# A planned MetaFormer layer on one core: the set-up work of the pipeline's filling, split and put elsewhere

## The chip, the cores and the metric

The kernel runs on one core of a Trainium2 chip. The metric is the device time of one execution in microseconds. The kernel before took 2755.74 us, the median of three runs (2751.01 to 2756.01). A core has five engines that work side by side, each in the order of its own instruction list: TensorE (PE, matmul; its weight loads are PEld), VectorE (DVE), ScalarE (ACT), GpSimd (POOL) and SyncE (SP). SP issues most transfers here, ACT the stores of intermediate results. An instruction waits, where it must, on semaphores, and everything behind it on the same engine waits with it.

## The reference

One layer over x of shape (8, 128, 128, 96): a Fourier token mixer, then a feed-forward network that rounds to small floats. What matters here:

```
x = x + conv(ln_c(x))                      # token mixer
t = x + ffn(ln_t(x))                       # 96 -> 384 -> 96
conv: x_pre = soa(ln(x) @ w1)              # 192 channels, relu, squared
      xf    = rfft2(x_pre)                 # per channel, over 128 x 128
      filt  = three filters, (16,9), (8,4), (24,13) coefficients,
              enlarged by cubic interpolation to (128, 65)
      r     = softmax(mlp(means of the image))    # mixes the three filters
      out   = irfft2(xf * sum(filt * r)) @ w2
ffn:  y = q_acc(q_acc(q_mul(x) @ q_mul(W)) + q_mul(b))   # q_mul: 5 exponent, 2 mantissa bits
```

All matmuls of the mixer are in float32. Everything that depends only on the parameters (the projection with batch norm folded in, the filters' enlarged rows, the rounded weights of the network) is computed on the chip at the start of each execution.

## The kernel before, in words

Each of the eight images goes through three streams. Stream a (`before`, the first pass): blocks of 16 columns are loaded (`load_x`, L802), their statistics taken (`measure`, L748; `variance`, `root`, `inverse`, `rest`, L753 to L782), the factors stored to DRAM (`store_r`, L815, buffer Rd) and loaded again spread over 96 partitions (`load_r`, L819, buffer rB, two of them). A transposed copy of x (`load_xT`, L811, four buffers zT with a row of ones below, so that the bias comes in with the matmul) is scaled by them (`scale`, L823), projected (`project`, L836, px), rectified and squared on ACT (L847, L854), transformed along one axis (`transform`, L865, py), folded on DVE (`fold`, L877, yst) and stored by ACT (`store_y`, L881, buffer Yd). When a whole image is through, its rates follow (`rate_v0` to `rate_n`). Stream s (`spectrum`) loads Yd and the filter rows T again, transforms along the other axis (`along_w`, L1059, pz), weighs and multiplies with the filters, mixes channels and transforms back. Stream c (`after`) finishes the inverse, adds the residual and runs the network. The streams of different images overlap; at the start there is only stream a of image 0.

The order is not that of the program text. Every step is handed to `at(time, function, ..., after=...)` with a wished place in time and the steps that it needs. `in_order` then walks through a model of the five engines, with the costs of the table `COST` (engine, time on it, time of its transfers), and takes on each engine the step that is ready and has the best score of place and delay. The outcome is a fixed order of instructions for every engine. The places of the streams come from `WINDOWS` and `OFFSETS`; the places of the set-up work from three constants, `T_WEIGHTS`, `T_CONST` and `T_ROWS`, on the same scale.

The set-up work is of four kinds. `make_weights` (L622) folds batch norm into the projection W1S (DVE, ACT, POOL and one matmul) and clears the ones rows of the four zT (`nc.gpsimd.memset`, L637). `others` (L639) makes small constants after eleven loads (L554). `rows` and `ends` (L682, L663) make the filters' rows with small matmuls; `row_put` and `end_put` (L690, L673) copy them out on DVE and, in the same step, issue two stores to T from SP (L695, L696, L678). `weights` (L698) issues four loads of the network's parameters from SP (L705 to L709) and, in the same step, six casts on DVE (L710 to L715). Since a step is put into the order as one, its loads stand on SP and its casts on DVE at the place where the planner took it.

A buffer that is to be filled again makes its new writer wait for the last reader: two of rB, two of xb, six of tk (row copies), two of te (end copies). Each transfer also waits, on its issuing engine, for an earlier transfer that used the same of eight completion semaphores.

Of the kernel before, what the change touches and what calls it, by code (L numbers as in the profile page):

```python
# [34 lines left out]
F32 = mybir.dt.float32  # L35
# [7 lines left out]
B, H, W, C = 8, 128, 128, 96  # L43
# [5 lines left out]
HID = 384  # L49
NHC = HID // 128  # L50
# [4 lines left out]
R = 2 * NW  # L55
# [7 lines left out]
NU = W // QW  # L63
PAIRS = [w for u in range(NU) for w in (2 * u, 2 * u + 1, 127 - 2 * u, 126 - 2 * u)]

T_WEIGHTS, T_CONST, T_ROWS = -112.0, 40.0, (-19.0, 94.0)

WINDOWS = {
    "a": ((-1016.3, 224.2), (1155.2, 782.6), (913.1, 640.2), (700.4, 97.1), (81, 722.9), (986.1, 683.8), (1759.7, 398.2), (2087.9, 538.4)),
    "s": ((159.4, 351.5), (85.6, 1024.7), (720.2, 346.4), (425.8, 331.2), (-126.3, 469.9), (-78, 205.3), (815.2, 257), (1827.2, 30.5)),  # L70
    "c": ((1028.7, 511.2), (1109.6, 188.3), (1290.9, 349.7), (1829.2, 439.1), (2176.6, 456.9), (2490.5, 149.5), (2420.5, 484.7), (2163.8, 1143.1)),
}
OFFSETS = {
    "a_context": -69.32,
# [19 lines left out]
    "a_root": -155.19,  # L94
    "a_scale": 83.17,
    "a_square": 92.51,
    "a_store_r": 12.56,
    "a_store_y": -218.91,
    "a_transform": -124.2,
    "a_variance": -11.06,  # L100
    "c_accumulated": -194.42,
    "c_add_up": -42.25,
    "c_bias": -232.6,
    "c_biased": -34.16,
    "c_first": -3.46,
# [6 lines left out]
    "c_measure": 206.09,  # L112
    "c_put8": 55.17,
    "c_quantise": 161.11,
    "c_quantise_v": 271.29,
    "c_residual": -76.16,
    "c_rest": -195.99,
    "c_root": 122.09,
# [8 lines left out]
    "s_alone_z": 223.71,  # L127
    "s_along_w": -28.38,
    "s_combine": -31.52,
    "s_copy_sr": 135.72,  # L130
    "s_filters_of": 27.98,
    "s_invert": 0.86,
    "s_inverted": -111.88,
# [22 lines left out]
PE, ACT, DVE, POOL, SP = range(5)  # L156
# [60 lines left out]
    "a_rate_n": (DVE, 4, 0),  # L217
    "_make_weights": (DVE, 7.4, 0),
    "_others": (DVE, 1.5, 1),
    "_weights": (DVE, 5, 2),  # L220
    "_ends": (PE, 2.2, 0),
    "_end_put": (DVE, 1.25, 1),
    "_rows": (PE, 1.2, 0),
    "_row_put": (DVE, 1.25, 1),
    "_next_pool": (SP, 0, 0),
    "a_load_x": (SP, 0.6, 1.92),
    "a_load_xT": (SP, 0.8, 1.05),
# [303 lines left out]
def metaformer_kernel(ctx: ExitStack, tc: tile.TileContext, a: dict, out: bass.AP):  # L531
    nc = tc.nc
# [11 lines left out]
    ops = []  # L544
# [61 lines left out]
    def projection(sp):  # L606


        raw = sp.tile([C, MED + SCTX + RHID], F32, name="raw")
        ident = sp.tile([128, 128], F32, name="ident")  # L610
        CEN = load(T_WEIGHTS, "CEN", [C, C], pool=sp)
        row = [C + 1, SCTX]
        bn = load(T_WEIGHTS, "bn", [C + 1, 4, SCTX], a["bn"].partition_broadcast(C + 1), sp)
        var, gam, mu, bet = (bn[:, i, :] for i in range(4))
        soa_scale = load(T_WEIGHTS, "soa1_scale", [128, 1], a["soa1_scale"].partition_broadcast(128), sp)
        bn_a = sp.tile(row, F32, name="bn_a")
        bn_t = sp.tile(row, F32, name="bn_t")

        def load_raw():
            nc.sync.dma_start(out=raw, in_=a["raw"])  # L620

        def make_weights():  # L622
            nc.vector.tensor_scalar(var, var, 1e-5, None, ALU.add)
            rsqrt(bn_a, var, bn_t)
            nc.vector.tensor_tensor(bn_a, bn_a, gam, ALU.mult)
            nc.vector.tensor_tensor(mu, mu, bn_a, ALU.mult)
            nc.vector.tensor_tensor(mu, bet, mu, ALU.subtract)
            pr = bank("pr")
            nc.tensor.matmul(pr[:C, : MED + SCTX + RHID], lhsT=CEN, rhs=raw, start=True, stop=True)
            nc.scalar.copy(W1S[:C, :MED], pr[:C, :MED])  # L630
            nc.vector.tensor_tensor(W1S[:C, MED:], pr[:C, MED : MED + SCTX], bn_a[:C, :], ALU.mult)
            nc.vector.memset(W1S[C:, :MED], 0.0)
            nc.vector.tensor_copy(W1S[C:, MED:], mu[C:, :])
            nc.scalar.copy(fc1a, pr[:C, MED + SCTX : MED + SCTX + RHID])
            nc.vector.tensor_scalar(F1, F1, soa_scale, None, ALU.mult)
            for t in zTs:
                nc.gpsimd.memset(t[C : C + 1, :, :], 1.0)  # L637

        def others():  # L639
            nc.vector.tensor_scalar(w2N, w2C, -1.0, None, ALU.mult)  # L640
            make_identity(nc, ident)
            nc.vector.tensor_copy(ident8, ident, saturate=False)
            nc.vector.memset(ones, 1.0 / (H * W))
            nc.vector.tensor_scalar(soa_bias, soa_bias, 128.0, None, ALU.mult)

        at(T_WEIGHTS, load_raw)
        loads = ("CEN", "bn", "soa1_scale", "F1", "load_raw")
        at(T_WEIGHTS + 0.1, make_weights, after=[(None, k) for k in loads], banks=1, until=[(None, "make_weights")])
        at(T_CONST, others, after=[(None, "soa1_bias"), (None, "w2C")])

    def filters(sp):
# [21 lines left out]
        def end_put(s, q):  # L673
            tk = sp.tile([L, 2, MED], F32, name="te", tag="te", bufs=2)
            nc.vector.tensor_copy(tk.rearrange("k r m -> k (r m)"), pts.pop(("end", s, q)))
            r0 = R + 4 * s + 2 * q
            for i in range(2):
                nc.sync.dma_start(out=T[i, r0 : r0 + 2, :, :].rearrange("r k m -> k r m"), in_=tk)  # L678

        pts = {}  # L680
# [9 lines left out]
        def row_put(i, s):  # L690
            (_, c, w0, n) = next(p for p in pieces[i] if p[0] == s)
            tk = sp.tile([128, 2, MED], F32, name="tk", tag="tk", bufs=6)
            nc.vector.tensor_copy(tk[:, :n, :].rearrange("k r m -> k (r m)"), pts.pop((i, s)))
            r0 = c * NW + WOFF[s] + w0
            nc.sync.dma_start(out=T[0, r0 : r0 + n, :, :].rearrange("r k m -> k r m"), in_=tk[:L, :n, :])  # L695
            nc.sync.dma_start(out=T[1, r0 : r0 + n, 1 : L - 1, :].rearrange("r k m -> k r m"), in_=tk[L:, :n, :])  # L696

        def weights():  # L698
            w1f = sp.tile([C, HID], F32, name="w1f")
            w2f = sp.tile([128, NHC, C], F32, name="w2f")  # L700
            b1f = sp.tile([128, NHC], F32, name="b1f")
            b2f = sp.tile([128, C], F32, name="b2f")
            b1h = sp.tile([128, NHC], F8, name="b1h")
            b2h = sp.tile([128, C], F8, name="b2h")
            nc.sync.dma_start(out=w1f, in_=a["W1T"])  # L705
            nc.sync.dma_start(out=w2f, in_=a["W2T"].rearrange("(n p) c -> p n c", p=128))
            with nc.allow_non_contiguous_dma("384 biases"):
                nc.sync.dma_start(out=b1f, in_=a["b1"].rearrange("(n p) -> p n", p=128))
            nc.sync.dma_start(out=b2f, in_=a["b2"].partition_broadcast(128))  # L709
            nc.vector.tensor_copy(W1q, w1f, saturate=False)  # L710
            nc.vector.tensor_copy(W2q, w2f, saturate=False)
            nc.vector.tensor_copy(b1h, b1f, saturate=False)
            nc.vector.tensor_copy(b2h, b2f, saturate=False)
            nc.vector.tensor_copy(b1q, b1h.unsqueeze(2).to_broadcast([128, NHC, QW * 128]))
            nc.vector.tensor_copy(b2q, b2h)  # L715
# [4 lines left out]
        ]  # L720
        n = max(len(p) for p in by_scale)
        pieces = [[p[i] for p in by_scale if i < len(p)] for i in range(n)]
        for i in range(n):
            t = T_ROWS[0] + (T_ROWS[1] - T_ROWS[0]) * i / n
            puts = [(None, "row_put", i, p[0]) for p in pieces[i]]
            at(t, rows, i, after=[(None, "load_scales")], banks=len(puts), until=puts)
            for k in puts:
                at(t + 1, row_put, i, k[3], after=[(None, "rows", i)])
        for s in range(NS):
            t = T_ROWS[1] + 1 + s  # L730
            puts = [(None, "end_put", s, q) for q in range(2)]
            at(t, ends, s, after=[(None, "load_scales")], banks=2, until=puts)
            for q in range(2):
                at(t + 0.5, end_put, s, q, after=[(None, "ends", s)])
        at(T_ROWS[1] + 5, weights, after=[(None, "row_put", n - 1, 2)])

    def named(what, b, n):

# [50 lines left out]
    def before(b, t0, P):  # L789
# [97 lines left out]
        for u in range(NU):  # L887
# [10 lines left out]
            if q % 2 == 0:  # L898
                hb = u // 2
                after = both("project", u - 2 * NZT) + both("project", u - 2 * NZT + 1)  # L900
                if b == 0:
                    after.append((None, "make_weights"))
                at(t - 0.003, load_xT, hb, after=after)
                at(t, load_r, hb, after=[one("scale", hb - 2), one("store_r", blk)])
                after = [one("load_xT", hb), one("load_r", hb)]
                at(t, scale, hb, after=after)
# [101 lines left out]
    def spectrum(b, t0, P):  # L1008
# [200 lines left out]
            kept_v[b] += 1  # L1209

        stored_y = [(("a", b), "store_y", u) for u in range(NU)]
        filled = [op.key for op in ops if b == 0 and op.key[1] in ("row_put", "end_put", "others", "GL", "GM", "SEL")]

        def mixer(g):

# [236 lines left out]
        pools["c"] = ctx.enter_context(tc.tile_pool(name="pc", bufs=2))  # L1452

    stream[0] = None
    at(T_ROWS[1] + 6, next_pool, after=[op.key for op in ops if op.key[0] is None])
    for op, banks in in_order(in_turn(ops)):
        free_banks[:] = banks
        op.what(*op.args)
# [52 lines left out]
```

## Time and profile before

| what | value |
|---|---|
| median of three runs | 2755.74 us (2751.01 to 2756.01) |
| the profiled execution's own time | 2760.28 us |
| its span in the profile | 2758.4 us |
| mean clock granted to PE | 0.942 |
| PE, DVE, ACT, POOL busy | 89%, 83%, 78%, 61% of the span |
| moved by transfers | 621.17 MB, 225 GB/s in the mean |
| first scaling (L823) | 34.85 us |
| first fold (L877) | 50.19 us |
| rates of image 0 begin (L928) | 211.28 us |
| first matmul of stream s (L1059) | 242.10 us |

The profile shows one execution. All times in it are microseconds from the span's start. A row of a group or of the order of time names the line of the kernel, the engine, the operation, the tile written and the tile read, and how many instructions it holds; the idle time before it stands in brackets, with what ended it. "SPq" and "ACTq" are the issuing of transfers. A stage's row gives for each engine the busy time in it, then the clock granted to PE as a share of the full one, the mean busy share of the 16 transfer engines and what they moved.

### The profile page before, as it was taken

The page shows a single profiled execution, that of the slowest core. Times are in us where ns is not written, and L with a number is a line of the kernel's source. Part 1 is how long each engine was busy: PE and PEld are TensorE (multiplying, and loading weights), DVE is VectorE, ACT ScalarE, POOL GpSimd, SP SyncE. Part 2 cuts the span into 40 slices and gives each one's busy share as a digit, 9 for nine tenths or more (in the row PEclk, how much of TensorE's full clock was granted, in tenths as well). Part 3 has the DMA queues.
Part 4 walks back from the last instruction along what each step waited for, and adds up shares of the span by engine and source line. Part 5 has one row for each costly group of instructions (what it writes and reads, how often), then busy time and mean ns, then how long its engine had stood idle before and what let it go on. Part 6 is the DMA issues. An engine that isn't in the chain of part 4 may idle for free.

```text
span 2758.4 us, 91912 instructions
## 1 busy us (share of the span) xinstructions
PE 2446.1 (89%) x37042; PEld 1784.2 (65%) x37042; DVE 2275.8 (83%) x5485; ACT 2143.0 (78%) x4332; POOL 1689.0 (61%) x2534
## 2 busy tenths in 40 slices
PE   5789999989989998999999999998999997988664
PEld 3456777766667766666677776766667675666332
DVE  5468788888889888988988988888979987878785
ACT  2255565648988788987998788988989888978875
POOL 3134455556567657755787576866766776777444
PEclk9699999999999999999999999999999998999775
DMA  7689889988866987588768988786768666564341
GB/s 211 200 265 283 270 276 290 290 267 269 260 209 220 297 260 218 187 255 248 223 199 253 291 260 247 230 252 200 234 190 250 191 206 185 153 218 150 116 136 46
DMA packets 506620, 621.17 MB, mean 225 GB/s; under 512 B 165838, under 2 KB 440551, under 8 KB 506171
## 3 DMA queue, kind: packets, MB, share of 16 engines
q1 hardware_dynamic: 418130, 464.28, 57.1%
q10 hardware_dynamic: 88064, 151.02, 15.2%
q8 instruction: 292, 4.78, 0.7%
q14 instruction: 134, 1.09, 0.1%
HBM read 407.03 MB, written 208.16 MB: 223 GB/s over the span
## 4 chain that ended last, share of the span: by engine, by line
PE 29%; ACT 13%; DVE 7%; issue 5%; POOL 3%; DMA 3%; POOLq 0%; ACTq 0%; SPq 0%; DVEq 0%
PE pv L1155 4%; ACT y L1346 3%; PE px L836 3%; PE pf L1074 3%; PE pk L1292 3%; PE pz L1059 3%; PE py L865 3%; ACT h L1359 3%; PE pg L1196 3%; PE po L1366 2%; PE ph L1339 2%; ACT z L1316 2%; DMA vin<-Vd 2%; DVE y L1350 1%; DVE t L1103 1%
## 5 line engine op out<-in xcount | busy, mean ns | idle before, releaser
L836 PE MATMUL px<-W1S,zT 97*128 97x240 f32 x2048 | 507.0, 382 | 27.2 <-DVE yst L877 12.3
L836 PEld LDWEIGHTS px<-W1S,zT 97*128 97x128 f32 x2048 | 395.7, 197 | 142.1 <-DVE yst L877 18.3
L865 PE MATMUL py<-X,F 128*128 128x384 f32 x1024 | 440.5, 519 | 21.1 <-DVE t L1298 3.8
L1044 POOL TENSOR_TENSOR tw<-tb,r 128x384 f32<-128x384 f32 (+1 forms) x264 | 288.3, 1092 | 277.2 <-PE pf L1074 131.5
L1346 ACT CAST y<-ph 128x512 f16<-128x512 f32 x768 | 416.7, 602 | 24.7 <-PE ph L1339 23.3
L847 ACT ACTIVATE rl<-px 128x480 f32<-128x480 f32 x512 | 292.2, 578 | 131.5 <-PE px L836 104.2
L1359 ACT ACTIVATE h<-y 128x1536 fp8e5<-128x1536 f16 (+1 forms) x256 | 370.3, 1447 | 24.7 <-DVE y L1350 21.1
L1316 ACT ACTIVATE z<-t,ln_m,ln_r 128x96 fp8e5<-128x96 f32 x848 | 360.8, 474 | 9.3 <-POOL ln_m L781 5.9
L1350 DVE TENSOR_TENSOR y<-y,b1q 128x1536 f16<-128x1536 f16 x256 | 319.9, 1250 | 52.5 <-ACT y L1346 51.5
L861 POOL TENSOR_TENSOR sacc<-sacc,rl 128x192 f32<-128x192 f32 x248 | 171.5, 692 | 293.0 <-ACT rl L847 287.0
L1155 PE MATMUL pv<-w2C,xf 64*64 64x96 f32 x9264 | 317.7, 247 | 30.3 <-issue 27.4
L877 DVE TENSOR_TENSOR yst<-py,yb 128x384 f32<-128x384 f32 x512 | 261.3, 545 | 76.4 <-PE py L865 25.5
L1155 PEld LDWEIGHTS pv<-w2C,xf 64*64 64x64 f32 x9264 | 275.6, 135 | 57.0 <-issue 40.7
L1097 DVE TENSOR_TENSOR d<-pz,sr 128x390 f32<-128x390 f32 x512 | 264.8, 553 | 44.1 <-ACT sr L1090 43.7
L1103 DVE TENSOR_TENSOR t<-d,pf 128x780 f32<-128x780 f32 x256 | 245.3, 958 | 61.9 <-PE pf L1074 31.0
L1339 PE MATMUL ph<-zT,W1q 96*128 96x512 fp8e5 x768 | 255.3, 407 | 32.8 <-ACT zT L1335 9.5
L1074 PE MATMUL pf<-RW,tw 64*128 64x130 f32 x3120 | 255.8, 293 | 26.3 <-DVE t L1108 9.7
L1117 POOL TENSOR_TENSOR xf<-t 128x390 f32<-128x390 f32 x256 | 235.1, 918 | 68.4 <-DVE t L1103 59.7
L1059 PE MATMUL pz<-F,yt 64*64 64x65 f32 x12480 | 252.9, 224 | 15.5 <-issue 7.7
L1074 PEld LDWEIGHTS pf<-RW,tw 64*128 64x128 f32 x3120 | 203.9, 190 | 90.4 <-issue 35.4
L1381 POOL TENSOR_TENSOR o<-o,b2q 128x1536 f16<-128x1536 f16 x64 | 201.4, 3147 | 93.8 <-ACT o L1377 92.9
L1059 PEld LDWEIGHTS pz<-F,yt 64*64 64x64 f32 x12480 | 219.5, 137 | 59.3 <-issue 18.2
(130 smaller groups left out, 5005.4 us busy)
## 6 DMA issues: line engine op xcount, KB each, us to landing
Yd<-yst ACTq DMA_DIRECT2D x256, 384.0 KB
yt<-Yd SPq DMA_DIRECT2D x248, 384.0 KB
xb<-in_xw SPq DMA_DIRECT2D x64, 768.0 KB
zT<-in_xT SPq DMA_DIRECT2D x128, 384.0 KB
rB<-Rd SPq DMA_DIRECT2D x128, 384.0 KB
tb<-T SPq DMA_DIRECT2D x256, 192.0 KB
Vd<-gst ACTq DMA_DIRECT2D x128, 384.0 KB
t<-in_x SPq DMA_DIRECT2D x64, 768.0 KB
```

Of the source, the lines that this page charges most:

```text
L836: nc.tensor.matmul(px[:, i * (MED + SCTX) : (i + 1) * (MED + SCTX)], lhsT=zTs[(b * NU // 2 + u // 2) % NZT][:, QW * (u % 2) + i0 + i, :], ...
L847: nc.scalar.activation(kept["rl", u][:, i0 : i0 + 2, :].rearrange("h w m -> h (w m)"), kept.pop(("px", u, i0)), AF.Relu)
L865: nc.tensor.matmul(py, lhsT=F1, rhs=kept["X", u][:, i0 : i0 + 2, :].rearrange("h w m -> h (w m)"), start=True, stop=True)
L1044: nc.gpsimd.tensor_tensor(tw[p, :].rearrange("p (q k m) -> p k q m", q=3, k=2), tb[p, :].rearrange(order, k=2, q=3), rates[b][p, :].rearra ...
L1059: nc.tensor.matmul(halves[i][64 * k : 64 * k + 64, c * L : (c + 1) * L], lhsT=kept["yt", g][rows, 2 * cs + k, 64 * q : 64 * q + 64], rhs=F ...
L1074: nc.tensor.matmul(pf[:, s, q * 2 * L : (q + 1) * 2 * L], lhsT=tw[p, 128 * q : 128 * q + 128], rhs=RW[p, :], start=True, stop=True,)
L1155: nc.tensor.matmul(kept["pv", p, r][half, i * C : (i + 1) * C], lhsT=kept["xf", g][rows, k, q, half], rhs=(w2N if k == 1 and h == 1 else w ...
L1316: nc.scalar.activation(z, t, AF.Identity, bias=m, scale=r, saturate=False)
L1339: nc.tensor.matmul(kept["ph", u, n], lhsT=W1q[:, n * 128 : (n + 1) * 128], rhs=kept["zT", u], start=True, stop=True)
L1346: nc.scalar.copy(kept["y", u][:, n, :], kept.pop(("ph", u, n)))
L1350: nc.vector.tensor_tensor(y, y, b1q, ALU.add)
L1359: nc.scalar.activation(h, y, AF.Relu, saturate=False)
```

## The change

Five edits, and numbers that move with them:

- The clearing of the ones rows becomes a step of its own, `fill_ones`, placed one unit ahead of the weights; the loads of zT for image 0 wait for it, no longer for `make_weights`.
- `make_weights` also needs the first `inverse` (the reciprocal of block 0's statistics).
- `T_CONST` goes from 40 to 100, and the first of `T_ROWS` from -19 to 0.
- The stores of rows and ends become steps of their own, `row_store` and `end_store`, and the copies name the steps that free their buffer and the copy before them.
- `load_w` (four loads) and `weights` (six casts) become two steps, with places at 154 and 254 instead of one at 99. W2 and b1 come in the layout in which they are used, so that their loads are contiguous.
- Some costs of the planner's table and some places in `WINDOWS` and `OFFSETS` change.

```diff
-T_WEIGHTS, T_CONST, T_ROWS = -112.0, 40.0, (-19.0, 94.0)
+T_WEIGHTS, T_CONST, T_ROWS = -112.0, 100.0, (0.0, 94.0)
...
-    "_weights": (DVE, 5, 2),
-    "_ends": (PE, 2.2, 0),
-    "_end_put": (DVE, 1.25, 1),
+    "_weights": (DVE, 2.9, 0),
+    "_load_w": (SP, 1.6, 1.5),
+    "_fill_ones": (POOL, 4.0, 0),
+    "_ends": (PE, 2.8, 0),
+    "_end_put": (DVE, 0.552, 0),
+    "_end_store": (SP, 0.7, 0.62),
...
-    "_row_put": (DVE, 1.25, 1),
+    "_row_put": (DVE, 0.552, 0),
+    "_row_store": (SP, 0.7, 0.62),
...
+
+        def fill_ones():
             for t in zTs:
                 nc.gpsimd.memset(t[C : C + 1, :, :], 1.0)
...
-        at(T_WEIGHTS + 0.1, make_weights, after=[(None, k) for k in loads], banks=1, until=[(None, "make_weights")])
+        at(T_WEIGHTS - 1, fill_ones)
+        at(T_WEIGHTS + 0.1, make_weights, after=[(None, k) for k in loads] + [(("a", 0), "inverse", 0)], banks=1, until=[(None, "make_weights")])
...
+            pts[i, s] = tk
+
+        def row_store(i, s):
+            (_, c, w0, n), tk = next(p for p in pieces[i] if p[0] == s), pts.pop((i, s))
             r0 = c * NW + WOFF[s] + w0
             nc.sync.dma_start(out=T[0, r0 : r0 + n, :, :].rearrange("r k m -> k r m"), in_=tk[:L, :n, :])
...
+        def load_w():
+            nc.sync.dma_start(out=w1f, in_=a["W1T"])
+            nc.sync.dma_start(out=w2f, in_=a["W2T"])
+            nc.sync.dma_start(out=b1f, in_=a["b1"])
+            nc.sync.dma_start(out=b2f, in_=a["b2"].partition_broadcast(128))
+
         def weights():
...
-            at(t, rows, i, after=[(None, "load_scales")], banks=len(puts), until=puts)
+            at(t, rows, i, after=[(None, "load_scales"), (None, "rows", i - 1)], banks=len(puts), until=puts)
             for k in puts:
-                at(t + 1, row_put, i, k[3], after=[(None, "rows", i)])
+                free = [(None, "row_put") + j for j in turn[-1:]] + [(None, "row_store") + j for j in turn[:-5][-1:]]
+                at(t + 1, row_put, i, k[3], after=[(None, "rows", i)] + free)
+                at(t + 1, row_store, i, k[3], after=[k])
+                turn.append(k[2:])
...
-        at(T_ROWS[1] + 5, weights, after=[(None, "row_put", n - 1, 2)])
+        at(T_ROWS[1] + 60, load_w)
+        at(T_ROWS[1] + 160, weights, after=[(None, "load_w")])
...
                 if b == 0:
-                    after.append((None, "make_weights"))
+                    after.append((None, "fill_ones"))
                 at(t - 0.003, load_xT, hb, after=after)
...
-        filled = [op.key for op in ops if b == 0 and op.key[1] in ("row_put", "end_put", "others", "GL", "GM", "SEL")]
+        filled = [op.key for op in ops if b == 0 and op.key[1] in ("row_store", "end_store", "others", "GL", "GM", "SEL")]
```

## Prediction

> **What bounds the kernel now.** First the totals: PE is busy 89% of the span, DVE 83%, no engine near 100%, so a share of the whole says little. The change touches only the filling of the pipeline, so I cut the span into stages (columns: stretch, its length, then busy time and instruction count for PE, PEld, DVE, ACT and POOL, PE clock granted, DMA share, GB/s):
>
> ```profile
> 0.00:36.00 36.00, 12.76 (x24) 5.78 (x24) 16.43 (x74) 2.67 (x7) 11.19 (x38) 1.00 0.69 185
> 36.00:90.00 54.00, 42.35 (x128) 27.71 (x129) 33.07 (x126) 22.28 (x41) 18.50 (x59) 0.79 0.82 249
> 90.00:130.00 40.00, 29.62 (x66) 14.89 (x66) 14.54 (x39) 9.02 (x15) 2.35 (x4) 0.60 0.55 163
> 130.00:170.00 40.00, 34.54 (x120) 22.21 (x119) 27.43 (x108) 17.95 (x34) 12.47 (x48) 0.87 0.88 280
> 170.00:242.00 72.00, 62.96 (x228) 44.49 (x226) 48.42 (x154) 44.40 (x79) 24.26 (x60) 0.88 0.80 248
> 242.00:300.00 58.00, 50.70 (x969) 39.76 (x970) 47.30 (x108) 27.51 (x55) 34.42 (x53) 1.00 0.99 302
> 300.00:400.00 100.00, 98.53 (x1113) 75.43 (x1112) 77.37 (x213) 68.83 (x125) 46.62 (x90) 1.00 0.88 273
> ```
>
> The first image's first pass runs alone up to 242 us, where the second stage's first matmul starts. From 242 to 300 the transfers are at their ceiling (0.99, 302 GB/s), from 300 PE is (98.5 of 100 us). Before 242 the transfers carry most, at 249 to 280 GB/s, except in 90 to 130: 163 GB/s, with every engine but PE nearly idle and PE itself on a clock of 0.60. That hole is the place to look. The instructions in order of time in it (start, duration; in brackets the idle time before and what ended it):
>
> ```profile
> 89.05 1.47 DVE L693 COPY tk<-pt 128x384 f32<-128x384 f32 x3
> ...
> 94.07 0.48 ACT L871 COPY yb<-py 128x384 f32<-128x384 f32 x1 [0.71 <-PE py L865]
> ...
> 98.11 0.37 SPq L705 DMA_DIRECT2D w1f<-in_W1T  x1
> ...
> 100.73 0.35 SPq L709 DMA_DIRECT2D b2f<-in_b  x1
> ...
> 102.02 0.36 DVE L710 CAST W1q<-w1f 96x384 fp8e5<-96x384 f32 x1 [11.49 <-DMA w1f<-in_W1T]
> ...
> 105.14 0.21 DVE L713 CAST b2h<-b2f 128x96 fp8e5<-128x96 f32 x1 [2.46 <-DMA b2f<-in_b]
> 105.26 1.75 DVE L714 CAST b1q<-b1h 128x1536 f16<-128x1536 fp8e5 x1
> 107.04 1.01 DVE L877 TENSOR_TENSOR yst<-py,yb 128x384 f32<-128x384 f32 x2
> ```
>
> DVE stands 11.49 us before the weight cast at L710, then 2.46 us at L713. The fold behind it (L877) had its inputs at 94.55 (94.07 + 0.48) and ran at 107.04, 12.5 us late. PE could not go on without that fold's bank (8.0 us of wait at L686, released by L877), ACT not without PE (12.1 us, the longest of L847).
>
> The very start, in the same view:
>
> ```profile
> 5.03 2.66 DVE L748 BATCH_NORM_STATS2 st<-xb 128x6 f32<-128x96 f32 x16 [5.03 <-DMA xb<-in_xw]
> ...
> 12.32 0.27 POOL L573 TENSOR_TENSOR bn_t<-bn_a 97x48 f32<-97x48 f32 x1 [11.89 <-DVE bn_a L568]
> ...
> 13.70 3.75 POOL L637 MEMSET zT<- 1x1024 f32 x4
> ...
> 17.53 0.24 POOL L758 TENSOR_TENSOR ln_d<-st 128x16 f32<-128x16 f32 x1
> ...
> 22.91 0.35 SPq L815 DMA_DIRECT2D Rd<-ln_r  x1
> ...
> 30.46 0.31 SPq L819 DMA_DIRECT2D rB<-Rd  x1
> ...
> 34.85 1.16 DVE L823 SCALAR_TENSOR_TENSOR zT<-zT,rB 96x1024 f32<-96x1024 f32 x1
> ```
>
> The statistics of the first block are done at 7.69 (5.03 + 2.66), yet POOL takes them up at 17.53: it waits 11.89 us for the batch-norm chain and then clears the ones rows. The factors go out at 22.91, come back from 30.46, and the first scaling, ahead of all projections, is at 34.85.
>
> **What the Trainium skill says.** "DMA: Bandwidth & Descriptors", Issuing engines are not separate DMA queues: what SP and ACT issue shares the same 16 engines. The trace agrees: SP's loads and ACT's Yd stores together stop at 302 GB/s, 0.99 busy; bytes count, not queues. The same page, Rules for kernel authors: issue a transfer early and wait for it late. The hole is the opposite: w1f issued at 98.11, after DVE began to wait at 90.5. "TensorE: Matmul & The Clock Gate", What's actually happening: after an idle window of about 3.4 us the array falls to half clock. The trace agrees: 0.60 here, and four projection matmuls take 1.97 us at 110 against 0.97 at 199; so the hole costs more than the wait.
>
> **The change, part by part.** I read the new order of instructions on each engine against the old. The same operations are issued; from about the 160th transfer of SP, the 330th instruction of DVE and the 210th of PE on, the order is the same but for single swaps. That join is at about 180 us of the trace before (the scalings at 181.24 and later). So the change shortens the stretch before the join, or does not, and the rest follows shifted.
>
> Weights. Load and casts become two operations. The four loads now stand 34th to 37th on SP (99th to 102nd before), the six casts behind the first scaling, long before the hole. Removed: 11.49 + 2.46 = 13.95 us of DVE's wait and the slow restart. Worked out over bytes: 90 to 130 moved 163 x 40 = 6.53 MB; the neighbours ran at (249 x 54 + 280 x 40) / 94 = 262 GB/s, so the same bytes take 24.9 us: 15.1 saved. At 249 it is 13.8, at the ceiling of 302 it is 18.4. The casts themselves, 0.36 + 0.30 + 0.16 + 0.21 + 1.75 + 0.20 = 3.0 us, move into a time when DVE waits for xb anyway (4.33 us before the statistics at 30.47); without that cover they cost 3.0. Their new wait: the last load takes 4.4 us (100.73 to 105.14), and issued at about 29 it lands at 33 to 34, against a first scaling that ends at about 33: 0 to 2 us. What is late next is the fourth block's statistics and the second scaling, which wait for transfers issued after b2f, so I take 0.
>
> Ones row. Four clearings, 3.75 us, go to POOL's idle start (hidden: POOL had 11.89 us of idle time there). The weight preparation waits for the first reciprocal. The first factors then come at: 7.7 statistics, 1.2 variance (17.53 to 18.72), 0.25 root, 0.25 reciprocal, i.e. 9.4; the batch-norm input lands at 10.17 as before, and POOL takes its four instructions (1.3 us) first, from about 11.0, since the table load of 1.28 us goes under its cover; then the last four (1.1 us): factors at 13.5 instead of 20.5, 7.0 earlier. The weights are then done at about 15 instead of 16.6, long before the first projection: no cost.
>
> SP's queue. Not all of the 7.0 us arrives. Rd is now 20th instead of 31st. Ahead of it zT and a second xb (1.15 MB, 4.4 us at 262) are put before the filter loads; each issue takes about 0.45 us and the large loads hold the ring until about 16, so Rd goes at about 18 (22.91). The eleven constants (0.45 us each, 5 us) were ahead of Rd; ten are now behind it, but nine of these, an xb and a zT are still ahead of the first rB: about 27 (30.46). With what is left of these and the rB itself to land, the first scaling comes at about 32: 3 us gained. Bounds: 7.0 above, and -2 below, if the second xb in front of the scales delays more than it prefetches.
>
> Row and end stores as own operations. 28 row stores and 6 end stores of two transfers each, same bytes, stand among SP's loads at other places (39th to 133rd instead of 29th to 142nd). SP waited 19.2 us in total for tk copies; separate stores let loads pass. The row matrices are needed only when the second stage reads T with the rates, at 232: no cost and no gain of its own. Contiguous W2 and b1: two small loads, inside the 4.4 us above.
>
> Sum: 15.1 + 3 = 18 us off the profiled 2760.28: 2742. The median of the runs shown is 4.5 lower; the same 18 off it: 2755.74 - 18 = 2738. That it carries to the end: after the join the order is the same, the transfers are at their ceiling to 300 and PE behind that, all released by data and not by a clock.
>
> **Rivals.** (a) More: with the hole gone and stores apart, all of 36 to 242 runs at the ceiling. It moves 13.4 + 6.5 + 11.2 + 17.9 = 49 MB, which at 302 GB/s is 162 us instead of 206: 44 at most, perhaps 35: 2721. For it: SP's wait for tk. Against: rB has two buffers, so every scaling waits a round trip, and PE was 92% busy in 50 to 70 at its lower clock. (b) Nothing: the stretch is held by bytes, which are the same, and what is gained early is waited for at the join: 0 to 5 us, 2753. Against it: the 163 GB/s. (c) Slower: the casts' wait isn't gone but moved. They stand on DVE ahead of the fourth block's statistics, the second scaling and the first folds, and SP issues their loads only behind the first rB, which waits for Rd. Each us that b2f is late is a us of the whole fill. It decides from 18 + 5.5 = 23.5 us of wait, b2f landing at about 57 instead of 34; at 30 us of wait the time is 2768. Against it: SP's longest single wait in the first 210 us is 9.0 us.
>
> **Numbers.** About 0.2% (5.5 us) is what a measurement here can tell from no change; three runs lay within 5.0. Chances: the forecast (8 to 28 us gained, 2728 to 2748) 0.68; (a) 0.13; (b) 0.12; (c) 0.07. Faster 0.81, same 0.12, slower 0.07. Range: from 2722, cutting part of (a), to 2752, most of (b), leaving out (c).
>
> **What would show it.** In the new profile: DVE idle less than 4 us ahead of W1q, which comes at 32 to 36; first scaling at 30 to 34; no stretch of 40 us between 36 and 220 under 220 GB/s; the first pz matmul of the second stage at about 224 instead of 242; from there the same stretches, shifted. Wrong would be a new wait of over 10 us on DVE or SP before 150, or a pz at 224 with an end that is not earlier: then the later stages gave it back.

## The result

The changed kernel took 2745.91 us in the median (20 executions, 2730.83 to 2762.29) beside 2756.38 us for the kernel before (20 executions, 2744.60 to 2776.73). The ratio is 0.9959, with a 95% interval of 0.9940 to 0.9977. A second series gave 0.9954 (0.9936 to 0.9972). By the medians 10.5 us are gained, 10.4 in the second series, and 6 to 18 by the intervals; 2738 was predicted, inside a range of 2722 to 2752.

One execution says little of so small a gain: the profiled one of the changed kernel took 2760.16 us (span 2758.3), as long as the profiled one of the kernel before. The filling is therefore compared by its own milestones, and the end by medians.

The stages of the changed kernel, same cuts and columns as before:

```profile
36.00:90.00 54.00, 42.51 (x142) 28.37 (x140) 35.54 (x130) 24.21 (x45) 18.06 (x56) 0.87 0.85 263
90.00:130.00 40.00, 35.75 (x118) 21.95 (x116) 20.28 (x50) 17.43 (x29) 6.94 (x16) 0.87 0.73 222
130.00:170.00 40.00, 27.17 (x78) 18.77 (x79) 27.81 (x120) 14.75 (x30) 13.83 (x47) 0.77 0.86 273
170.00:242.00 72.00, 62.41 (x329) 44.19 (x328) 47.77 (x135) 41.47 (x73) 24.35 (x55) 0.89 0.85 255
242.00:300.00 58.00, 51.62 (x855) 39.76 (x856) 45.06 (x118) 26.34 (x54) 30.92 (x56) 0.91 0.86 254
```

The hole is gone: 90 to 130 moves 222 GB/s where it moved 163, PE is busy 35.75 us instead of 29.62, its clock is 0.87 instead of 0.60. DVE, in order of time:

```profile
33.55 1.22 DVE L846 SCALAR_TENSOR_TENSOR zT<-zT,rB 96x1024 f32<-96x1024 f32 x1 [1.62 <-DMA rB<-Rd]
...
34.70 0.35 DVE L726 CAST W1q<-w1f 96x384 fp8e5<-96x384 f32 x1
...
88.25 1.02 DVE L900 TENSOR_TENSOR yst<-py,yb 128x384 f32<-128x384 f32 x2 [5.40 <-ACT yb L894]
```

The cast L726 has no bracket: it waits for nothing, where L710 waited 11.49 us. The first scaling is 1.3 us earlier (34.85 before), the eighth 17.0 us (107.97 to 90.93). Then some is lost again: the last of the first nineteen is 12.9 us earlier, the first pz matmul 11.0 (242.10 to 231.09), and the work at 320 us 5.5. The line at 88.25 shows a wait that is new, 5.40 us behind ACT.

### The profile page after: what moved, and what is told of

Its sections match the earlier page's. It is cut to its first block, busy times and chain, and to the rows that moved or that the text cites. A ratio compares the mean times of both kernels' runs of the same rounds, so it can differ in the third digit from the quotient of the medians.

```text
span 2758.3 us, 91920 instructions
## 1 busy us (share of the span) xinstructions
PE 2448.1 (89%) x37042; PEld 1786.2 (65%) x37042; DVE 2274.0 (82%) x5485; ACT 2141.8 (78%) x4332; POOL 1689.6 (61%) x2534
## 3 DMA queue, kind: packets, MB, share of 16 engines
q10 hardware_dynamic: 88064, 151.02, 15.2%
## 4 chain that ended last, share of the span: by engine, by line
PE 54%; ACT 16%; DVE 11%; DMA 7%; issue 7%; POOL 4%; SPq 0%; ACTq 0%; POOLq 0%; DVEq 0%
PE px L859 11%; PE py L888 9%; PE pv L1178 7%; PE pf L1097 5%; PE pz L1082 5%; PE pg L1219 5%; PE pk L1315 5%; ACT y L1369 4%; ACT h L1382 4%; PE ph L1362 3%; PE po L1389 3%; ACT z L1339 2%; DMA vin<-Vd 2%; DVE y L1373 2%; DVE st L771 2%
## 5 line engine op out<-in xcount | busy, mean ns | idle before, releaser
L859 PEld LDWEIGHTS px<-W1S,zT 97*128 97x128 f32 x2048 | 398.1, 198 | 132.9 <-DVE yst L900 15.2
```

Source lines behind the costliest of these rows:

```text
L859: nc.tensor.matmul(px[:, i * (MED + SCTX) : (i + 1) * (MED + SCTX)], lhsT=zTs[(b * NU // 2 + u // 2) % NZT][:, QW * (u % 2) + i0 + i, :], ...
```

## The experiments

All are compared in the same two ways: the start of the first pz matmul in the profile (242.1 us in the kernel before), and the ratio of times to the kernel before in the same series, with its 95% interval.

| kernel | first pz, us | ahead, us | ratio (interval) |
|---|---|---|---|
| before, second profile | 241.7 | 0.4 | |
| the change | 231.1 | 11.0 | 0.9959 (0.9940 to 0.9977) |
| the change, again | 221.5 | 20.6 | 0.9954 (0.9936 to 0.9972) |
| before, loads early | 229.5 | 12.6 | 0.9982 (0.9963 to 1.0002) |
| before, ends early | 234.8 | 7.3 | 0.9998 (0.9976 to 1.0020) |
| before, both early | 226.9 | 15.2 | 0.9979 (0.9958 to 1.0000) |
| before, front of SP's queue only | 248.7 | -6.6 | 1.0016 (0.9998 to 1.0035) |
| change, weights back | 226.6 | 15.5 | 0.9955 (0.9937 to 0.9973) |
| change, ends late | 231.8 | 10.3 | 0.9960 (0.9941 to 0.9979) |
| change, both back | 230.7 | 11.4 | 0.9968 (0.9952 to 0.9985) |
| change, ones row back | 227.4 | 14.7 | 0.9946 (0.9929 to 0.9962) |
| change, stores back | 224.7 | 17.4 | 0.9933 (0.9912 to 0.9954) |
| change, stores back, more rB | 219.8 | 22.3 | 0.9944 (0.9929 to 0.9958) |

**Second profiles.** Both kernels unchanged.

> The changed kernel once more, for a second profile. Theory: the 17 us that the filling has gained by the eighth scaling are partly given back for a reason that returns in each execution (transfers at their ceiling between the join and 315 us). Then the rates begin at 197 to 200 us again, the first pz matmul comes at 229 to 233, and at 320 us the work stands only 4 to 7 us ahead of the kernel before. Rival: the loss behind the first pz is chance of one execution; then the lead at 320 us is 10 us or more this time. Time of both theories: 2743 to 2749 us.

> The kernel before once more, for a second profile. Theory: its slow stretch belongs to its order of work, not to one execution. Then the rates begin within 5 us of 211.28 again, DVE waits 8 to 16 us for w1f and b2f, and 110 to 130 us, behind that wait, again moves less than 170 GB/s with PE at a clock under 0.65. Rival: the first profile was a slow draw in the filling; then the rates begin at 205 us or earlier, and part of the 13 to 22 us of lead that the changed order showed there was chance.

The filling of the kernel before repeats: the rates begin at the same place to 0.3 us, DVE waits 10.27 and 3.27 us, and 110 to 130 us moves 159 and 148 GB/s. That of the changed kernel does not: its second profile is 9.6 us further ahead at the first pz, and at 320 us it leads by 15, not 5.5. So the loss behind 231 us was chance of one execution, and the theory of a loss that returns is out. Two profiles of the changed order can differ by 10 us: the single profiles below are read with that in mind.

**The wait alone.** In the order before, the four loads move:

```diff
+        if op.key == (("a", 0), "load_r", 1):
+            early[0]()        # issues the loads of w1f, w2f, b1f, b2f; the casts stay
```

> The order before, with one thing moved: the four loads of the network's parameters are issued ahead of the second load of factors instead of behind the last filter row; their casts stay where they were. Theory (the hole is the wait for these loads): DVE waits less than 1 us ahead of W1q, 90 to 130 us moves 215 GB/s or more, the first scaling stays at 34 to 36, the rates begin 11 to 15 us earlier than 211.28, at 196 to 200, and the time is 6 to 12 us under the kernel before, ratio 0.9956 to 0.9978. Rival (the gain comes from the front and from the stores standing by themselves): the rates begin at 206 or later and the ratio is 0.9985 to 1.001, since the four loads only push other bytes back.

The wait is gone (W1q at 88.13 without one, instead of 102.02), and the first pz comes 12.6 us earlier, close to the 15.1 reckoned; the ratio, 0.9982, leaves 0 to 10 us for the end and is not clear of 1. Three expectations failed. The ratio lies above the 0.9978 expected at most. The first scaling comes at 32.96 us, 1.9 earlier than in the kernel before, though nothing ahead of it was moved: so much can one profile's first scaling differ. And 90 to 130 us moves only 200 GB/s, because its second half stayed as it was:

```profile
100.00:110.00 10.00, 8.77 (x17) 3.01 (x17) 5.31 (x13) 1.89 (x3) 1.27 (x1) 0.63 0.82 257
110.00:120.00 10.00, 10.00 (x19) 4.78 (x18) 2.40 (x10) 1.62 (x3) 0.59 (x1) 0.50 0.54 163
120.00:130.00 10.00, 10.00 (x31) 5.85 (x31) 5.43 (x14) 4.05 (x8) 1.57 (x6) 0.85 0.49 147
```

From 110 to 130 PE is busy all the time, at half clock at first, and the transfers are busy only half of it. What PE does there is read from its own list. First the kernel before, then the changed one:

```profile
36.16 5.47 PE L836 MATMUL px<-W1S,zT 97*128 97x240 f32 x16 [9.77 <-POOL ln_d L573]
...
119.31 5.38 PE L669 MATMUL pt<-cw,re 16*65 16x384 f32 x8
...
129.21 2.79 PE L669 MATMUL pt<-cw,re 8*65 8x384 f32 x8
...
137.37 2.79 PE L669 MATMUL pt<-cw,re 24*65 24x384 f32 x8
```

```profile
23.40 1.54 PE L676 MATMUL pt<-cw,re 16*65 16x384 f32 x2
...
24.74 10.71 PE L676 MATMUL pt<-cw,re 16*65 16x384 f32 x22
35.38 5.17 PE L859 MATMUL px<-W1S,zT 97*128 97x240 f32 x12
```

The 24 matmuls of the end rows, 5.38 + 2.79 + 2.79 = 10.96 us of PE, stood in the middle of the filling. In the run with the loads early they take 5.38 us at 104.63, 5.38 at 114.72 and 2.79 at 125.34; projections and transforms fill the rest. In the changed order the 24 stand ahead of the first projection, where PE had stood idle for 9.77 us in the kernel before. The prediction had not seen this move.

**Weights back.** The changed order, with loads and casts together again:

```diff
+    for key in ("load_w", "weights"):
+        move((None, key), (("a", 0), "fold", 6, 0))      # to ahead of this step
```

> The changed kernel, with the four loads and the six casts put back to one place, ahead of the fold of block 6. Theory: DVE waits 10 to 15 us for w1f and b2f again, one stretch of 20 us falls under 170 GB/s, the rates begin at 208 to 213 instead of 198, and nearly all of the gain is gone: ratio to the kernel before 0.998 to 1.0005. Rival (front and stores carry the gain): the rates begin at 203 or earlier and the ratio stays at 0.995 to 0.997.

The wait came back and cost nothing that shows. The cast and four stretches of 10 us:

```profile
82.62 0.35 DVE L726 CAST W1q<-w1f 96x384 fp8e5<-96x384 f32 x1 [8.21 <-DMA w1f<-in_W1T]
```

```profile
80.00:90.00 10.00, 3.58 (x10) 1.76 (x12) 6.85 (x16) 1.67 (x3) 1.41 (x5) 0.51 0.48 136
90.00:100.00 10.00, 9.82 (x46) 5.55 (x40) 9.84 (x32) 5.18 (x10) 2.16 (x7) 1.00 0.87 272
100.00:110.00 10.00, 9.53 (x36) 5.39 (x34) 5.64 (x13) 4.71 (x9) 1.46 (x5) 1.00 0.86 276
110.00:120.00 10.00, 9.21 (x28) 5.44 (x28) 5.85 (x12) 3.62 (x7) 1.18 (x2) 0.85 0.88 263
```

A hole of 10 us at 136 GB/s is there, but behind it the stretch is clear, PE at a clock of 1.00 and the transfers at 263 to 276 GB/s; the sixth scaling comes at 71.9 us, the seventh at 86.3 and the eighth at 92.1 (75.6, 79.7 and 90.9 in the changed kernel): the wait shows at the seventh and is made up by the eighth. The first pz comes at 226.6. The rates begin at 193.9 and the ratio is 0.9955, both as the rival had them; the theory's 208 to 213 and 0.998 or more failed. A wait of this kind is thus not worth its length in itself.

**The ends alone, and from both sides.** In the changed kernel the ends wait for the last rows again; in the kernel before their wished place goes ahead of the rows:

```diff
-after=[(None, "load_scales"), (None, "ends", s - 1)]                        # change
+after=[(None, "load_scales"), (None, "rows", n - 1), (None, "ends", s - 1)]
-            t = T_ROWS[1] + 1 + s                                           # before
+            t = T_ROWS[0] - 10 + s
```

> The changed kernel, where the matmuls of the end rows wait for the last rows again, so that they stand in the second half of the filling as before and not ahead of the first scaling. Theory E (the 24 matmuls of the ends, 10.96 us of PE in the middle of the filling of the kernel before, were the larger part of its slow stretch): a stretch of 10 to 20 us with PE at 0.65 or less and under 180 GB/s comes back, the rates begin at 199 to 205 us, where the four profiles with early ends have 189 to 198, and the ratio to the kernel before is 0.997 to 0.9995. Theory W (the wait for the network's parameters was the slow stretch, as predicted): nothing changes, rates at 189 to 198, ratio 0.994 to 0.997.

> The kernel before, where the end rows are made ahead of the rows, in front of the first scaling; loads and casts of the network's parameters stay together behind the last row. Theory E: although DVE still waits 8 us or more for w1f and b2f, no stretch of 20 us behind it falls under 180 GB/s, the rates begin at 199 to 206 us instead of 211.28, ratio 0.996 to 0.9985. Theory W: the rates begin at 208 to 213 and the ratio is 0.9985 to 1.001.

Early ends in the order before move the first pz by 7.3 us, although DVE still waits 8.45 and 2.28 us for the loads; the time shows no gain (0.9998). The first scaling comes 3.6 us later there (38.41), and 100 to 120 us still moves only 183 and 163 GB/s. Since the planner then also puts the rows elsewhere, this is not the ends by themselves. Late ends in the changed order bring back ten microseconds at half clock and 123 GB/s:

```profile
120.00:130.00 10.00, 10.00 (x16) 3.19 (x15) 1.77 (x4) 0.84 (x1) 0.69 (x4) 0.50 0.42 123
```

The rates begin at 199.4 us as theory E had it, but the ratio stays at 0.9960, and 231.8 lies inside the spread of the changed kernel's own two profiles. Neither theory is carried by both measures.

**Both together.**

> The kernel before with these two edits alone: the four loads ahead of the second load of factors, the ends in front of the first scaling. Theory (two causes): the first pz matmul at 222 to 228 us, where the loads alone gave 229.5 and the ends alone 234.8, and a ratio of 0.993 to 0.997, as the whole change has it. Rival (the two gains are the same microseconds): the first pz matmul at 228 to 232 and a ratio of 0.9965 to 0.999.

> The changed kernel with both undone: the ends behind the last rows and the loads and casts of the network's parameters together, ahead of the fold of block 6. Theory (the slow stretch had two causes, DVE's wait for the loads and the ends' matmuls on a slow PE, and each by itself is partly caught up): the first pz matmul comes at 236 to 242 us, 0 to 6 ahead of the kernel before, and the ratio is 0.998 to 1.001. Rival (the lead comes from elsewhere, from the front, the constants or the order of rows): the first pz matmul at 226 to 232 and a ratio of 0.994 to 0.997, as with either undone alone.

Both early in the order before: 15.2 us ahead, as theory had it, but a ratio of 0.9979 (0.9958 to 1.0000), which is the rival's. The lead is less than the sum of the two alone (12.6 + 7.3 = 19.9), with one profile of each. The stretch of 110 to 130 us, 163 and 147 GB/s with the loads alone, is filled:

```profile
110.00:120.00 10.00, 7.57 (x20) 4.42 (x19) 5.80 (x15) 2.95 (x6) 2.24 (x7) 0.68 0.97 280
120.00:130.00 10.00, 9.13 (x40) 6.46 (x39) 8.66 (x33) 6.55 (x11) 3.03 (x11) 0.98 0.79 228
```

Both back in the changed order: still 11.4 us ahead and 0.9968, the rival's numbers. As an account of the whole gain, the theory of two causes fell. DVE's wait is shorter there (9.07 us, and none for b2f), which, counted in full, accounts for 4.9 of the 11.4.

**The rest: the front?** In the order before, the loads and constants at the head of SP's queue as the change has them; the row stores stay where they were:

```diff
+    for key in ((a0, "load_xT", 0), (a0, "load_x", 1)):
+        move(key, (None, "load_scales"))                           # to ahead of it
+    move((a0, "load_xT", 1), (None, "load_scales"), ahead=False)
+    for key in ("fc2T", "mlp", "SEL", "F2", "RW", "soa1_bias", "w2C", "GL", "GM", "GK"):
+        move((None, key), (a0, "load_r", 0))
```

> The kernel before, with only the front of SP's queue as the change has it: the first zT and the second xb ahead of the filter loads, the second zT behind them, and ten constants behind the first store of factors. Both undone together still left the first pz matmul 11.4 us ahead of the kernel before, of which 4.9 us (9.07 instead of 11.49 + 2.46 of DVE's wait) is the shorter wait. Theory F (the rest is the front): the first scaling at 31 to 34 us, the first pz matmul at 234 to 238, 4 to 8 ahead, ratio 0.997 to 0.9995. Theory R (the rest is that the changed order spreads the rows thinner, 3 copies instead of 7 ahead of the first scaling and 9 instead of 13 by the fourth): the first scaling gains up to 3 us, but the first pz matmul stays at 239 to 243, ratio 0.9985 to 1.001.

Both theories missed: the filling is slower, and the time shows no gain (1.0016). The run did not make the front of the change. The ten constants now stand directly ahead of the first rB, and eight row stores still stand ahead of them, where the change has none ahead of rB. The first rB goes at 31.32 instead of 30.46 (28.12 in the change), the first scaling comes at 36.93. So it does not say what the whole front is worth.

The traces themselves show where the rest of the lead arises. These are the seventh scalings of the kernel before, of the change, and of the change with both undone:

```profile
87.03 1.16 DVE L823 SCALAR_TENSOR_TENSOR zT<-zT,rB 96x1024 f32<-96x1024 f32 x1
```

```profile
79.69 1.21 DVE L846 SCALAR_TENSOR_TENSOR zT<-zT,rB 96x1024 f32<-96x1024 f32 x1
```

```profile
77.70 1.52 DVE L846 SCALAR_TENSOR_TENSOR zT<-zT,rB 96x1024 f32<-96x1024 f32 x1
```

The way from the first scaling to the seventh takes 52.2 and 51.6 us in the two profiles of the kernel before and 50.4 to 52.0 in the four orders built on it. It takes 46.1 and 45.5 in the change, 45.1 with both undone, and 44.5 to 48.2 in the other orders built on the change, but for the one whose put-back wait falls into it (53.9). Some 6 us of the lead are thus made before 90 us, ahead of the hole, and they stay when the loads, the ends or the ones row are put back. What makes them is open. The changed order spreads the rows thinner: between the two scalings it has 4 row copies, where the kernel before has 10. But the change with late ends has 8 there and is no slower (46.1 us), so the number of copies by itself does not account for the 6 us. No run changed the place of the rows alone.

**Ones row and stores.** Each of the two edits undone by order alone:

```diff
+    for key in ("make_weights", "fill_ones"):
+        move((None, key), (("a", 0), "variance", 0))     # to ahead of this step
```

> The changed kernel, with the clearing of the ones rows and the preparation of the weights put back ahead of the first variance on POOL. Theory (the front is worth little, since what follows it is held by bytes and by the round trip of the factors): the first scaling comes 2 to 5 us later than 33.55, the eleventh scaling less than 3 us later than 102, and the time is within 3 us of the changed kernel, ratio to the kernel before 0.995 to 0.997. Rival (each us at the front is a us at the end): the first scaling, the rates and the end all come 3 to 7 us later, ratio 0.997 to 0.9985.

The factors are then late again, and no loss shows:

```profile
13.80 3.75 POOL L643 MEMSET zT<- 1x1024 f32 x4
...
20.64 0.35 SPq L838 DMA_DIRECT2D Rd<-ln_r  x1
28.31 0.42 SPq L842 DMA_DIRECT2D rB<-Rd  x1
```

In the changed kernel Rd goes at 18.96 and rB at 28.12. Clearing the ones rows ahead of the statistics costs 1.7 us on Rd and 0.2 us on rB, because between the two SP has nine constants, an xb and a zT to issue. The first scaling is 0.12 us later (33.67), not the 2 to 5 expected, and the ratio is 0.9946. (The 102 us in the expectation is the change's tenth scaling; here the tenth comes at 97.7.)

```diff
+    for key in [op.key for op, _ in order if op.key[1] in ("row_store", "end_store")]:
+        move(key, (None, key[1].replace("store", "put")) + key[2:], ahead=False)
```

> The changed kernel, with each store of a row or an end directly behind its copy again, as one operation would put it. Theory (as predicted, stores by themselves are worth nothing): rates at 189 to 198 us, ratio to the kernel before 0.994 to 0.997. Rival (SP no longer stands at tk copies with loads behind them, and this is the gain): SP's waits for tk before 200 us grow by 10 us or more, rates at 203 or later, ratio 0.998 to 1.0005.

As predicted, no worth of the stores by themselves shows: with each store back behind its copy the rates begin at 192.7 and the ratio is 0.9933, not to be told from the change's 0.9959 by the intervals.

**One more buffer.**

```diff
-pa.tile(..., tag="rB")
+sp.tile(..., tag="rBs", bufs=3) if b == 0 and hb < 9 else pa.tile(..., tag="rB")
```

> The changed kernel with stores directly behind their copies, and for the first nine half blocks of image 0 three buffers for the spread factors rB instead of two, taken from the space of the set-up work. SP waits 37 to 40 us in 30 to 190 for a scaling to free rB, with loads of xb and zT queued behind. Theory (this wait holds back the transfers): it falls below 20 us, the first pz matmul comes at 212 to 220 us, ratio to the kernel before 0.989 to 0.9925. Rival (bytes and the next wait, for zT, take its place): the first pz matmul at 221 to 229, ratio 0.9925 to 0.9965.

The wait did not shrink (40.7 us). All of it lies behind 90 us, where the two old buffers are still used: the run did not touch what it meant to. What it says is that no gain of three buffers in the first 90 us shows in the time, 0.9944. This kernel and the one with stores back are both faster than the kernel before; neither can be told from the change.

## Why the prediction was right, and where its steps were not

**The place was right, its price nearly.** The change does fill the hole at 90 to 130 us. Removing the wait alone gives 12.6 us at the first pz, where 15.1 were reckoned by bytes and 13.95 by the waits themselves. The casts' new wait was taken as 0: it is 0, with W1q at 34.70. That the time fell into the forecast is still in part luck: at the end the wait alone gives a ratio of 0.9982, 0 to 10 us, and some 6 us of the lead come from the stretch between the first and the seventh scaling, for which the prediction had nothing.

**The step that failed is the reading of that hole as one thing.** The prediction put all of 90 to 130 down to the wait and a "slow restart" of PE behind it. The loads moved alone left 110 to 130 at 163 and 147 GB/s, with PE busy throughout: a second limit, PE itself, at half clock up to 122 us and with the ends' matmuls among its work. Nor did the half clock go with the wait: with the wait gone, and no gap of PE over 0.74 us, it was still 0.50. The row of 90 to 130 in the prediction already had PE busy for 29.62 of 40 us, and DVE, called nearly idle, for 14.54. And where it said "no cost and no gain of its own" of the row and end stores, it looked at the stores only; in the new order the ends' matmuls, too, had gone to where PE idles. Reading which instructions filled PE at 119 to 140 in the kernel before, and where they stand after, would have shown it. Nor is it shown that the gains add: 12.6 and 7.3 became 15.2, and the changed order with both undone kept 11.4. Having the wait back in that order showed no cost, so the reason for the gain that was written down is not the only one, and others can stand in for it.

**The front** was reckoned at 3 us and gave 1.3 at the first scaling, 1.5 in the second profile, of which the ones row has 0.12. Since the order before has its first scaling at 34.85, 34.04 and, with the loads early, 32.96, even this is not clear of chance. The factors were ready at 15.3, not 13.5, because the batch-norm input came at 11.88 and not at 10.17 as before. The times on SP were close (Rd 18.96 for 18, rB 28.12 for 27); the step that was wrong is crediting them to POOL's earlier factors. SP's queue sets rB: with factors 5 us later it went at 28.31.

**The sum** of 18 us is above the end's 10.5 and just outside both intervals (6.3 to 16.5 and 7.7 to 17.6). At the first pz, 224 was predicted: the two profiles have 231.1 and 221.5, 226.3 in the mean, 15.8 ahead. That all of it carries to the end is thus not confirmed: the medians of the end keep 10.5. From the first pz to the end the profiled executions took 2516.3 and 2515.7 us before, 2527.2 and 2509.4 after; over all profiles it is 2509 to 2523 in the order before and 2509 to 2532 in the changed one. No steady loss or gain behind the first pz shows. For the three orders built on the kernel before with a lead at the first pz, the ratios give 5, 0.6 and 6 us for leads of 12.6, 7.3 and 15.2; for those built on the change the gain lies nearer the lead. Whether the single swaps of the later order make that difference stays open; so does why one order's filling repeats to 0.4 us and the other's does not.

**The rivals.** More (a), everything at the ceiling: 36 to 190 us moved 254 and 266 GB/s in the two profiles (234 before), not 302. Nor is 302 a ceiling for every mix of transfers: 377 to 387 us of the kernel before moved 382. Nothing (b) is excluded by the intervals, though its thought, that what is gained early is waited for later, fits the run with weights back, where an 8 us wait was made up by the second scaling behind it. Slower (c) did not happen: the loads had landed when they were wanted. Of the signs of failure, no wait of over 10 us appeared. Of the signs of success, one was missed: the changed kernel still has a stretch of 40 us under 220 GB/s (87 to 127 us, 211).

## What to carry to other kernels

When a stage has a hole, list what fills each engine through all of it, not only the wait that opens it: another engine can be the limit in its second half. Before pricing a removed wait, ask whether the stage can catch up behind it; price edits that act on the same stretch together, since their gains may overlap. Compare where every group of instructions stands before and after a reordering, also those that the edit does not name.

## What was not expected of the hardware

PE's clock fell to half while PE was working. The order before with the loads early, stretches of 2 us:

```profile
100.00:102.00 2.00, 1.34 (x5) 0.81 (x6) 0.73 (x1) 0.57 (x1) 0.33 (x1) 1.00 0.77 234
102.00:104.00 2.00, 1.43 (x4) 0.50 (x2) 0.77 (x3) 0.48 (x1) 0.94 (x1) 0.63 0.91 294
104.00:106.00 2.00, 2.00 (x5) 0.54 (x4) 1.26 (x3) 0.84 (x1) 0.00 (x0) 0.50 0.68 231
...
120.00:122.00 2.00, 2.00 (x4) 1.17 (x4) 0.22 (x1) 0.29 (x1) 0.00 (x0) 0.50 0.21 56
```

Its longest gap from 82 us on is 0.74 us, PE is two thirds busy when the clock drops, and then, as the profile counts it, busy 2.00 of 2.00 at 0.50 until 122. The times of the matmuls agree: eight of the ends take 5.38 us at 104.63 and at 114.72, and 2.79 us at 125.34, where the clock is full again. The Trainium skill's "TensorE: Matmul & The Clock Gate", What's actually happening, gives about 3.4 us of idleness for the drop and about 3.4 us of sustained work for the return. Here neither holds: no such idle window, and some 18 us of unbroken work at half clock. The measurement decides; whether a property of these matmuls (some are 8 and 16 rows deep) keeps the clock low was not tried.

ACT's store of Yd can hold ACT itself. In the changed kernel ACT stands from 81.70 us on. The store goes out at 86.71, and the activation queued behind it starts 5.58 us late; by the profile, an earlier store of Yd ended this wait:

```profile
87.28 0.57 ACT L870 ACTIVATE rl<-px 128x480 f32<-128x480 f32 x1 [5.58 <-DMA Yd<-yst]
```

DVE's wait of 5.40 us at 88.25 hangs on it.
